# The opening of a grouped-convolution and scan kernel: weights folded ahead, x in small pieces on two queues, and lone edges in the first pairs

## The chip, the core and the metric

The kernel runs on one core of a Trainium2 chip, in float32. The metric is the device time of one execution in microseconds (us). Its engines are TensorE (PE, with its weight loads as PEld), VectorE (DVE), ScalarE (ACT), GpSimd (POOL) and SyncE (SP), which issues most DMAs; ScalarE's queue can issue DMAs too. All times in this document are us, most of them from the start of the span.

## The reference

x has 4 images of 128 channels, 96 by 96. It is group-normalised (32 groups over channels and pixels, no learned scale), read as four sequences (rows, rows backwards, columns, columns backwards), and each sequence goes through the same block. The four results are fused by one matrix and added to x.

```python
t = grouped1x1(x, in_proj_w, in_proj_b, 4)            # 128 -> 512
u, gate = t[:, :256], t[:, 256:]
u = depthwise_conv(silu(u), dw_w, taps=5)
s = ssm_in_w @ u                                      # 256 -> 32
a = 0.999 + 0.0009 * sigmoid(ssm_delta_w @ u + ssm_delta_b)
bb, cc = tanh(ssm_b_w @ u + ssm_b_b), tanh(ssm_c_w @ u + ssm_c_b)
h = exp(P) * cumsum(bb * s * exp(-P)), P = cumsum(log a)   # h = a * h + bb * s
u = u + ssm_out_w @ (cc * h + ssm_d * s)
u = grouped1x1(u * sigmoid(gate), mix_w, mix_b, 4)
y = out_proj_w @ u + out_proj_b                       # 256 -> 128
out = x + fuse_w @ concat(y of the 4 sequences) + fuse_b
```

## The kernel before

**Phases, steps, pairs, units.** The work is 8 phases: image 0 by columns ("V"), image 0 by rows ("H"), image 1, and so on. A phase runs two sequences of opposite direction at once (s = 0 and 1). It has 6 steps of 16 lines; each step is cut into 4 interleaved residues p, taken in the order `TURN = (1, 2, 3, 0)`. One residue of one sequence is a *unit* of 384 positions; the two units of a residue are a *pair* t, 24 to a phase and 192 in all. `pair(t)` issues the first `LAG` = 6 pairs, `pair_on(t)` the others, `tail()` the end. `start()` is the opening, up to the point where the first projection can be issued. In these functions the order of the code is the order on each engine (a manual schedule). The loads ahead of them (`load_x` with its statistics, the weights) are ordered by the scheduler.

**The opening.** x of image 0 arrives in pieces on SyncE's queue; each 384 columns (a chunk, 0.197 MB, 24 in all) get a `bn_stats` on VectorE (L329). `stats_first` then yields the normalisation step by step: aggregate, product with `gmean` for the group means, product for the variances, square root and reciprocal (`inv`), the scaled input weights `wn`, and their biases `bn` from products of the *scaled* weights with the means. Between its steps `start` issues fillers (L1163, products of x with itself that nobody reads) and the fold of the output weights: `outer` (L1170) forms fuse_w times out_proj_w for four directions (`w_of`), `inner` (L1178) multiplies mix_w in (`w_fin`). Three further products with vectors give the fused bias `b_fin` (L1252).

**In-projection and SiLU.** `burst(j, g)` is the in-projection of residue g: channel half j, both sequences; `silus(j, g)` its SiLU on ScalarE (L509). `sils[step]` holds the results of a step. For later steps `front(t + R)` in pair t does the same, one residue a pair, four pairs ahead. `load_front` refills `x_in` behind it, row by row as the in-projection has read them: `x_in` has one buffer per sequence.

**The depthwise convolution** of a unit: channel half 0 on TensorE (`conv` with the matrices `band`, then `conv_less` with `less` for the neighbouring columns, then a copy of the result to `u`, L904), channel half 1 as five `taps` on VectorE (L728) with the first on ScalarE (L726). For residues 0 and 3 the part of `conv_less` is a single tap (`alone(p)`); `pair_on` then calls `add_lone` instead: one VectorE instruction (L675) that adds the shifted edge rows from the tile `lone` to the convolution and writes `u`. `keep_lone` writes a step's edge rows (32 partitions, four DMAs) to DRAM, and `load_lone` reads them back in the other layout. Before, the pairs 0 to 5 always use `conv_less`.

**Projection, scan, output.** `proj` (L130 psum<-u,main) computes b, c, delta and s; the scan runs on VectorE one step later; `out_of` adds ssm_out to a copy of u that `under` put into PSUM; `gating` multiplies by the gate; `accumulate` applies `w_fin`. Phase 2 of an image reads back what phase 1 kept in DRAM: `keep_silu` writes the SiLU results of step 0 (four DMAs of 770 KB, one a residue), `kept` the gates.

**Statistics of the next image** come from chunks `xs` that `load_chunks` fetches and `stats_chunks` reads: before, one in each of the pairs 2 to 5, then two in every pair of residues 3 and 0.

**DMA order.** A DMA queue runs its transfers in order of issue. The program has eight DMA semaphores, used in turn over all queues: a ninth transfer is issued only when the one that had its semaphore has landed, and the issuing engine waits for that in its own order.

Of the kernel before, what the change touches and what calls it, by code (L numbers as in the profile page):

```python
# [42 lines left out]
F32 = mybir.dt.float32  # L43
# [4 lines left out]
P = 128  # L48
# [8 lines left out]
R = 4  # L57
# [11 lines left out]
def conv_preact_kernel(  # L69
# [95 lines left out]
    stats, free = {}, [FRONT[1]]  # L165
# [10 lines left out]
    def stats_first(b):  # L176
# [11 lines left out]
        gm4 = sp.tile([P, 4], F32, tag="gm4", name=f"gm4_{b}")  # L188
        nc.vector.tensor_scalar_mul(gm4, gmask, mean)
# [18 lines left out]
        stats[b] = (wns, bn)  # L208
        yield
        pb = bank(free[0])  # L210
# [114 lines left out]
    def load_x(chunks):  # L325
        for c, n in chunks:
            nc.sync.dma_start(accf[:, bass.ds(c * SC, n * SC)], xr[b0, :, bass.ds(c * SC, n * SC)])
            for e in range(c, c + n):
                nc.vector.bn_stats(stats_of(b0)[:, e, :], accf[:, bass.ts(e, SC)])  # L329
# [11 lines left out]
    nc.scalar.activation(first_table, first_table, AF.Sqrt)  # L341
    w_small = load(small, "small", nc.scalar)
    load_x([(0, 1), (1, 1), (2, 1), (3, 2), (5, 2), (7, 3), (10, 4), (14, 4), (18, 4), (22, 2)])
    w_out_fuse = shared()
    nc.sync.dma_start(w_out_fuse[:, 0 : 2 * HID + 4 * P], fuse)
# [36 lines left out]
    for s in range(2):  # L382
# [13 lines left out]
    nc.gpsimd.tensor_scalar_mul(b_proj[64:P, 0:1], b_proj[64:P, 0:1], 0.5)  # L396
    nc.gpsimd.tensor_scalar_mul(
        w_proj[:, :, 2 * MH : 3 * MH], w_proj[:, :, 2 * MH : 3 * MH], 0.5
    )
# [10 lines left out]

    def chunks_of(t):

        un = units[min(2 * t, NU - 2)]
        st, k = divmod(t % NP, R)
        if t < LAG:
            return [(b0 + 1, t - 2)] if t > 1 else []
        if un["order"] == "V" and un["b"] + 1 < B and k > 1:
            return [(un["b"] + 1, 4 * st + 2 * (k - 2) + e) for e in range(2)]
        return []
# [11 lines left out]
    def stats_chunks(t):  # L431
        for b, c in chunks_of(t):
            nc.vector.bn_stats(stats_of(b)[:, c, :], chunks.pop((b, c)))
# [914 lines left out]
```

## Time and profile before

| | |
|---|---|
| three runs | 1741.92, 1742.92, 1745.32; median 1742.92 |
| profiled execution | 1742.22 |
| its span | 1740.4 |
| granted TensorE clock | 1.0 throughout |
| TensorE, VectorE, ScalarE, GpSimd busy | 99%, 87%, 86%, 83% |
| first `bn_stats` | 3.64 |
| fillers | 11.64 to 20.38 |
| mean product on TensorE | 20.31 |
| first SiLU | 24.46 |
| projections of pairs 0 to 6 | 34.93, 41.81, 48.59, 56.03, 63.92, 70.68, 79.30 |

Rows of a timeline show start, length, engine, line, operation and tiles; x14 after a row is a count of equal instructions that follow each other. One float32 product shows as two passes, so that seven fillers are fourteen rows. A helper such as `mm` (L130) records most products, so they are told apart by their tiles: `psum<-u,main` is a projection, `psum<-sil,band` a convolution, `psum<-sil,less` its second part, `psum<-x_in,wn` an in-projection, and L539 a gate.

### The profile page before, as it was taken

Reading aid. Unit: us, or ns where it says so; the run is one execution under the profiler, and the core shown is the slowest. Engines: PE = TensorE matmul, PEld = TensorE weight load, DVE = VectorE, ACT = ScalarE, POOL = GpSimd, SP = SyncE. Lnnn points to the kernel's source line nnn. Section 1 sums busy time; section 2 is a strip of 40 time slices with the busy share of each in tenths; the row PEclk is TensorE's granted clock in tenths of the full one; section 3 lists DMA queues with packets and bytes.
Section 4 is the critical chain, followed back from the end, with each engine's and each line's share of the span. In section 5 each row is a group of like instructions: output and inputs, shape, how many; then the busy total and the mean of one; then the engine's idle time right before and its main releaser. Section 6 shows DMA issues by size and latency. Waiting matters only on the chain.

```text
span 1740.4 us, 54418 instructions
## 1 busy us (share of the span) xinstructions
PE 1719.8 (99%) x22662; PEld 648.0 (37%) x22662; DVE 1509.2 (87%) x1508; ACT 1494.9 (86%) x2543; POOL 1449.3 (83%) x1496
## 2 busy tenths in 40 slices
PE   7999999999999999999999999999999999999998
PEld 3333333333333433344333443334333343334333
DVE  6899988888889998888889999888888888888887
ACT  4788888889888898888988888888998888888875
POOL 3589889888778988988787988898878889887887
PEclk9999999999999999999999999999999999999999
DMA  7755965368984786337896488433897549743365
GB/s 240 220 160 199 291 189 158 109 218 272 283 276 154 244 277 199 117 122 244 267 304 232 149 301 255 147 120 133 287 287 251 179 138 294 213 136 133 146 227 166
DMA packets 175908, 362.68 MB, mean 208 GB/s; under 512 B 16688, under 2 KB 150320, under 8 KB 175664
## 3 DMA queue, kind: packets, MB, share of 16 engines
q1 hardware_dynamic: 175520, 359.17, 64.5%
q8 instruction: 179, 2.93, 0.7%
q14 instruction: 65, 0.53, 0.1%
q10 hardware_dynamic: 144, 0.04, 0.0%
HBM read 220.62 MB, written 138.53 MB: 206 GB/s over the span
## 4 chain that ended last, share of the span: by engine, by line
PE 93%; DVE 2%; POOL 2%; ACT 1%; DMA 1%; issue 1%; SPq 0%; POOLq 0%; DVEq 0%; ACTq 0%
PE psum L130 79%; PE psum L559 8%; PE psum L539 6%; DVE psum L728 1%; PE psum L1163 1%; POOL acc L859 1%; DMA acc<-in_xr 0%; DVE u L622 0%; POOL t L809 0%; ACT psum L573 0%; ACT psum L726 0%; DVE u L728 0%; ACT sil L509 0%; DMA edge<-sil 0%; POOL t L810 0%
## 5 line engine op out<-in xcount | busy, mean ns | idle before, releaser
L728 DVE SCALAR_TENSOR_TENSOR psum<-sil,small,psum 128x768 f32<-128x768 f32 x576 | 589.0, 1023 | 43.5 <-ACT psum L726 18.3
L130 PE MATMUL psum<-u,w_fin 128*32 128x384 f32 (+1 forms) x6192 | 541.6, 485 | 1.1 <-DVE acc L857 0.5
L130 PE MATMUL psum<-u,main 128*32 128x384 f32 x6144 | 535.1, 489 | 0.7 <-DVE u L904 0.6
L622 DVE SCALAR_TENSOR_TENSOR u<-gate,psum 128x768 f32<-128x768 f32 x376 | 341.7, 950 | 151.2 <-PE psum L559 49.6
L859 POOL TENSOR_TENSOR acc<-ys,acc 128x384 f32<-128x384 f32 x375 | 416.5, 1132 | 14.7 <-DMA acc<-in_xr 1.9
L809 POOL TENSOR_TENSOR t<-t,t 64x384 f32<-64x384 f32 (+1 forms) x192 | 282.2, 1470 | 72.3 <-DVE t L803 50.1
L130 PEld LDWEIGHTS psum<-u,w_fin 128*32 128x32 f32 x6192 | 196.4, 110 | 308.4 <-issue 234.5
L573 ACT COPY psum<-u 128x768 f32<-128x768 f32 x383 | 300.6, 799 | 11.4 <-DVE u L622 4.9
L130 PEld LDWEIGHTS psum<-u,main 128*32 128x32 f32 x6144 | 180.4, 110 | 323.3 <-issue 217.2
L130 PE MATMUL psum<-sil,band 128*32 128x384 f32 x3072 | 285.6, 489 | 0.0
L776 POOL TENSOR_SCALAR t<-tm 64x384 f32<-64x384 f32 x184 | 172.5, 938 | 116.1 <-ACT tm L765 104.0
L810 POOL TENSOR_TENSOR t<-t,t 64x384 f32<-64x384 f32 (+1 forms) x192 | 233.9, 1218 | 15.1
L777 POOL TENSOR_TENSOR t<-t,tm 64x384 f32<-64x384 f32 x192 | 211.2, 1100 | 28.4 <-ACT t L768 13.7
L559 PE MATMUL psum<-t,main 32*128 32x384 f32 x1536 | 229.0, 525 | 3.2 <-ACT psum L573 3.2
L726 ACT ACTIVATE psum<-sil,small 128x768 f32<-128x768 f32 x191 | 172.4, 903 | 67.0 <-DVE u L622 62.3
L728 DVE SCALAR_TENSOR_TENSOR u<-sil,small,psum 128x768 f32<-128x768 f32 x192 | 194.9, 1015 | 6.8
L509 ACT ACTIVATE sil<-psum,bnorm 128x385 f32<-128x385 f32 x384 | 191.8, 584 | 4.6 <-PE psum L130 2.2
L539 PE MATMUL psum<-x_in,wn 32*128 32x384 f32 x768 | 164.0, 500 | 0.0
L842 ACT COPY ys<-psum 128x384 f32<-128x384 f32 x286 | 131.5, 477 | 28.8 <-PE psum L130 25.1
L130 PEld LDWEIGHTS psum<-sil,band 128*32 128x32 f32 x3072 | 88.8, 108 | 171.9 <-issue 63.0
L765 ACT ACTIVATE tm<-psum,small 128x384 f32<-128x384 f32 x192 | 110.9, 578 | 15.8 <-PE psum L130 6.6
L559 PEld LDWEIGHTS psum<-t,main 32*128 32x128 f32 x1536 | 94.6, 183 | 75.8 <-issue 41.2
(109 smaller groups left out, 1527.3 us busy)
## 6 DMA issues: line engine op xcount, KB each, us to landing
gate<-kept SPq DMA_DIRECT2D x114, 768.0 KB, 5.9
kept<-gate SPq DMA_DIRECT2D x74, 768.0 KB, 3.6
sil<-sil SPq DMA_DIRECT2D x64, 770.0 KB, 7.6
lone<-edge SPq DMA_DIRECT2D x39, 770.0 KB, 8.3
x_in<-in_xs SPq DMA_DIRECT2D x250, 96.2 KB, 3.3
edge<-sil SPq DMA_DIRECT2D x96, 192.5 KB, 4.3
out<-acc SPq DMA_DIRECT2D x46, 384.0 KB, 7.3
acc<-in_xr SPq DMA_DIRECT2D x39, 384.0 KB, 6.8
```

Source lines behind the costliest of these rows:

```text
L130: nc.tensor.matmul(o[r, : rhs.shape[-1]], lhsT, rhs, start=start, stop=stop, skip_group_check=True)
L509: nc.scalar.activation(sils[step][:, s, j, g, :], bank(bk)[:, : N + 1], AF.Silu, bias=bn[:, 1:2] if j else bn[:, 4 + g : 5 + g],)
L539: nc.tensor.matmul(bank(to)[:, :N], stats[un["b"]][0][r, s, :], x_in[s][r, q, off : off + N], start=True, stop=True)
L559: nc.tensor.matmul(bank(ssm(bi, s) + j)[:, :N], w_so[r, bass.ts(j, P)], z[r, :], start=(bi, s) not in seeded, stop=True, skip_group_check= ...
L573: nc.scalar.copy(psum[:, ssm(bi, s) : ssm(bi, s) + 2, :N], us[bi][:, s])
L622: nc.vector.scalar_tensor_tensor(v, g, 1.0, pz, ALU.add, ALU.mult)
L728: nc.vector.scalar_tensor_tensor(us[i][:, :, 1, :] if k == K - 1 else part, src, w_tap[:, k : k + 1], part, ALU.mult, ALU.add,)
L776: nc.gpsimd.tensor_scalar(*decay(i))
L777: nc.gpsimd.tensor_mul(ta[0:64, p, :], tb[0:64, :], tm[0:64, :])
L809: engine.tensor_mul(ta[0:64, p, r], tb[64:P, r], ta[64:P, p, r])
L810: engine.tensor_add(tb[0:64, r], ta[0:64, p, r], tb[0:64, r])
L859: adder.tensor_add(part, y, part)
```

## The change

The change has two parts.

In the opening: `fuse` is loaded first, by ScalarE's queue; x comes in 15 pieces of one or two chunks, in turn by SyncE and ScalarE, with the small weights after the fourth. `outer` and `inner` stand at the front of `start`, two directions a bank, and ScalarE copies their results. Four fillers stand ahead of the mean product (seven before), one and the three products of `b_fin` between mean and variance product. The biases are products of the *unscaled* weights with mean x inv. The order of bursts, SiLUs, taps and convolution in `start` is new.

In the pairs: `keep_lone(0)` and `load_lone(0)` stand at the end of `start`, and the pairs 2 and 3 use `add_lone`. `keep_silu(0, g)` moves from the end of `start` into the pairs 0, 1 and 2. `under` no longer leaves out unit pair 0. The chunks of image 1 move from the pairs 2 to 5 to the pairs 5 and 20 to 22 (three in 22).

```diff
 def stats_first(b):
...
-        wn = wns[:, 0, :]
+        shift = sp.tile([P, 1], F32, tag="dev", name=f"shift_{b}")
+        nc.vector.tensor_mul(shift, mean, inv[:, 0:1])
+        pb = bank(free[0])
+        for g in range(4):
+            for q in range(R):
+                mm(pb[:, 4 + g : 5 + g], q, w_in[0:32, 0, 32 * g : 32 * g + 32], shift[0:32, :], True, True)
...
-        product(pb[:, 0:4], wn, gm4)
-        for g in range(4):
-            for q in range(R):
-                mm(pb[:, 4 + g : 5 + g], q, wn[0:32, 32 * g : 32 * g + 32], mean[0:32, :], True, True)
-        nc.vector.tensor_sub(bn, b_in, pb[:, 0:8])
+        product(pb[:, 0:4], w_in[:, 0, :], gm4)
+        nc.vector.tensor_sub(bn[:, 0:4], b_in[:, 0:4], pb[:, 0:4])
...
+    def load_x(ends):
+        for e, (c, to) in enumerate(zip([0] + ends, ends)):
+            cols = bass.ds(c * SC, (to - c) * SC)
+            (nc.scalar if e % 2 else nc.sync).dma_start(accf[:, cols], xr[b0, :, cols])
+            if e == 3:
+                load_small()
+            for k in range(c, to):
+                nc.vector.bn_stats(stats_of(b0)[:, k, :], accf[:, bass.ts(k, SC)])
...
-    nc.sync.dma_start(w_out_fuse[:, 0 : 2 * HID + 4 * P], fuse)
+    nc.scalar.dma_start(w_out_fuse[:, 0 : 2 * HID + 4 * P], fuse)
+    load_x([1, 2, 3, 4, 6, 8, 10, 12, 14, 16, 18, 20, 22, 23, 24])
...
+        if ph == 0:
+            places = singles[2:] * 2 + [LAG - 1, NP - 4, NP - 3, NP - 2]
...
     def under(bi, s):
-        if bi + s == 0:
-            return
...
     def pair(t):
-            conv(i, banks)
-            conv_less(i, banks, False)
-            for s in range(2):
-                nc.vector.tensor_copy(us[i][:, s, 0, :], bank(min(banks) + s)[:, :N])
+            single = alone(units[i]["p"])
+            conv(i, banks, single)
+            if single:
+                add_lone(i, banks)
+            else:
+                conv_less(i, banks, False)
+                for s in range(2):
+                    nc.vector.tensor_copy(us[i][:, s, 0, :], bank(min(banks) + s)[:, :N])
...
-        if t == 2:
-            keep_lone(0)
...
+        for g in {0: (0,), 1: (1, 2), 2: (3,)}.get(t, ()):
+            keep_silu(0, g)
...
     def start():
+        nc.scalar.activation(first_table, first_table, AF.Sqrt)
+        outer((0, 1), 2)
+        outer((2, 3), 3)
+        inner((0, 1), 4)
+        inner((2, 3), 5)
...
-        for n in (512, 512, 512):
-            filler(n)
-        next(pieces)
         for n in (512, 512, 512, 512):
             filler(n)
         next(pieces)
-        outer(0, 0, nc.scalar.copy)
-        outer(1, 1, nc.scalar.copy)
         next(pieces)
-        outer(2, 4, nc.scalar.copy)
+        filler(512)
+        pf = bank(3)
...
-        inner((0, 1), 0)
-        inner((2, 3), 1)
...
-        for g in range(R):
-            keep_silu(0, g)
...
+        keep_lone(0)
+        load_lone(0)
```

What the edit does to the order on the engines shows at three places. First ScalarE from the program's first instruction to the first SiLU; `acc` is x, `shared` holds the fuse weights and their fold. Before:

```order
L322 DMA small<-in_small 128x86
L341 ACT_TABLE_LOAD
L341 ACTIVATE first_table<-first_table 128x1
L1174 COPY shared<-psum 128x256 x2
L198 ACTIVATE std<-var_253 128x2
L200 ACT_TABLE_LOAD
L200 ACTIVATE first_table<-std 128x1
L1174 COPY shared<-psum 128x256
L509 ACTIVATE sil_293<-psum,bnorm_266 128x385 x16
```

And now:

```order
L348 DMA shared<-in_fuse 128x1024
L330 DMA acc<-in_xr 128x384 x2
L324 DMA small<-in_small 128x86
L330 DMA acc<-in_xr 128x768 x4
L330 DMA acc<-in_xr 128x384
L1200 ACT_TABLE_LOAD
L1200 ACTIVATE first_table<-first_table 128x1
L1189 COPY shared<-psum 128x512 x2
L1198 ACTIVATE w_fin<-psum 128x512 x2
L1219 ACTIVATE b_fin<-psum,small 128x1
L196 ACTIVATE std<-var_276 128x2
```

Nine transfers now stand ahead of the table load and of the first copy of the fold. Then TensorE over the same stretch, before:

```order
L1163 MATMUL psum<-acc 128x512 x7
L130 MATMUL psum<-mv_221,gmean 32x1 x4
L1170 MATMUL psum<-shared 128x128 x4
L130 MATMUL psum<-ex_235,gmean 32x1 x8
L1170 MATMUL psum<-shared 128x128 x4
L1163 MATMUL psum<-acc 128x128
L130 MATMUL psum<-gm_0_237,wn_263 32x4 x4
L130 MATMUL psum<-mean_231,wn_263 32x1 x16
```

And now (`mv` and `ex` are the inputs of the mean and the variance product, `shift` is mean x inv):

```order
L1185 MATMUL psum<-shared 128x128 x8
L1193 MATMUL psum<-shared 128x128 x8
L1178 MATMUL psum<-acc 128x512 x4
L130 MATMUL psum<-mv_251,gmean 32x1 x4
L1178 MATMUL psum<-acc 128x512
L1218 MATMUL psum<-small,shared 128x1 x3
L130 MATMUL psum<-ex_261,gmean 32x1 x8
L130 MATMUL psum<-shift_283,main 32x1 x16
```

The fold moved ahead of the fillers; a filler and the bias products took its place between the mean and the variance product. Last, SyncE's queue from the end of `start` into the pairs, before:

```order
L489 DMA sil_0_202<-sil_293 512x1x385
L489 DMA sil_1_203<-sil_293 512x1x385
L489 DMA sil_2_204<-sil_293 512x1x385
L489 DMA sil_3_205<-sil_293 512x1x385
L427 DMA xs_0_437<-in_xr 128x384
L297 DMA x_in_70<-in_xs 32x385
L297 DMA x_in_71<-in_xs 32x385
```

And now:

```order
L672 DMA edge_0_212<-sil_308 32x4x385 x4
L678 DMA lone_440<-edge_0_212 128x4x385
L299 DMA x_in_70<-in_xs 32x385
L299 DMA x_in_71<-in_xs 32x385
L317 DMA x_in_70<-in_xs 64x385
L503 DMA sil_0_204<-sil_308 512x1x385
L299 DMA x_in_70<-in_xs 32x385
L299 DMA x_in_71<-in_xs 32x385
L317 DMA x_in_71<-in_xs 64x385
L503 DMA sil_1_205<-sil_308 512x1x385
L503 DMA sil_2_206<-sil_308 512x1x385
```

The four edges and the read of `lone`, which waits for them, stand in front of the `sil` writes, and these stand between the loads of `x_in` for step 2.

More of the change, by code (lines that the diff above doesn't have):

```diff
@@ L1191, in start @@
         next(pieces)
[L1192 to L1193 removed]
         next(pieces)
[L1195 removed]
+        filler(512)
+        pf = bank(3)
+        terms = [(w_of[:, 0, j, :], b_mix[:, j : j + 1]) for j in range(2)] + [(w_fuse[:, 0, :], b_out)]
+        for i, (lhsT, rhs) in enumerate(terms):
+            nc.tensor.matmul(pf[:, 0:1], lhsT, rhs, start=(i == 0), stop=(i == len(terms) - 1))
+        nc.scalar.activation(b_fin, pf[:, 0:1], AF.Identity, bias=b_fuse)
         next(pieces)
[L1197 to L1200 removed]
+        next(pieces)
         sils[0] = wk.tile([P, 2, 2, 4, N + 1], F32, tag="sil", name="sil_0")
```

106 lines of the change are left out of this document (50 added, 56 removed).

## The prediction

> **What bounds the kernel now.** All times are us from the start of the span. I read the page first: its busy times and the shares of the chain that ended last.
>
> ```profile
> PE 1719.8 (99%) x22662; PEld 648.0 (37%) x22662; DVE 1509.2 (87%) x1508; ACT 1494.9 (86%) x2543; POOL 1449.3 (83%) x1496
> PE 93%; DVE 2%; POOL 2%; ACT 1%; DMA 1%; issue 1%; SPq 0%; POOLq 0%; DVEq 0%; ACTq 0%
> ```
>
> TensorE is busy for 99% of the span and carries 93% of the chain, so whatever lets its queue run earlier in the opening comes off the end, unless TensorE has to wait again behind it. The diff touches the opening and pairs 0 to 6, so next came the chain of waits over the first 80 us (start, length, what):
>
> ```profile
> 3.62 7.98 DMA acc<-in_xr
> 11.64 8.73 PE psum L1163 x14
> 55.43 0.56 DVE u L904
> 59.37 3.60 DMA x_in<-in_xs
> 63.11 3.60 PE psum L130 x48
> ```
>
> x loads until 11.60 (a part of it; the rest hides), then seven fillers of two passes each hold TensorE until 20.37, with the product of the means right behind. From there the chain is TensorE's own but for two places: in pair 3 it waits for the copies of u, and in pair 4 for x_in, which lands at 59.37 + 3.60 = 62.97. Then the windows by stage: mean product to first SiLU, first SiLU to first projection, and pair by pair, each from its projection to the next (window, length, PE, PEld, DVE, ACT, POOL, clock, DMA share, GB/s).
>
> ```profile
> 20.31:24.46 4.15, 4.15 (x107) 3.62 (x114) 2.18 (x11) 2.69 (x6) 0.00 (x0) 1.00 0.79 185
> 24.46:34.93 10.47, 10.47 (x202) 5.78 (x184) 6.17 (x17) 8.98 (x19) 3.17 (x4) 1.00 0.35 89
> 34.93:41.81 6.88, 6.88 (x104) 2.30 (x100) 5.70 (x7) 5.83 (x11) 1.94 (x2) 1.00 1.05 288
> 41.81:48.59 6.78, 6.78 (x104) 2.19 (x100) 5.03 (x7) 5.61 (x12) 3.13 (x3) 1.00 1.09 201
> 48.59:56.03 7.44, 6.81 (x104) 2.15 (x100) 5.33 (x8) 4.99 (x10) 3.17 (x3) 1.00 0.86 252
> 56.03:63.92 7.89, 7.48 (x100) 2.23 (x100) 6.76 (x9) 6.90 (x13) 3.12 (x3) 1.00 0.84 233
> ```
>
> TensorE fills every window but 0.6 of the fifth and 0.4 of the sixth. From 34.93 on the transfers are nearly saturated too (share 0.84 to 1.09), and that second bound decides this forecast.
>
> **Part 1, up to the mean product (20.31 now).** The statistics and TensorE's fillers must both be over. In the answers below are the statistics, four weight loads of the fillers, SyncE's waits before an issue, ScalarE's table load and copies, and the second fold product.
>
> ```profile
> 11.62 6.67 DVE L329 BATCH_NORM_STATS2 bn<-acc 128x6 f32<-128x384 f32 x14 [0.41 <-DMA acc<-in_xr]
> 18.32 0.81 DVE L178 BATCH_NORM_AGGREGATE mv<-bn 128x2 f32<-128x144 f32 x1
> 10.00:11.00 1.00, 0.00 (x0) 0.00 (x0) 1.00 (x3) 0.00 (x0) 0.93 (x3) 1.00 1.03 418
> 15.22 0.33 PEld L1163 LDWEIGHTS psum<-acc 128*128 128x128 f32 x1 [0.52 <-issue]
> 16.07 0.33 PEld L1163 LDWEIGHTS psum<-acc 128*128 128x128 f32 x1 [0.52 <-issue]
> 16.78 0.19 PEld L1163 LDWEIGHTS psum<-acc 128*128 128x128 f32 x1 [0.38 <-issue]
> 17.21 0.19 PEld L1163 LDWEIGHTS psum<-acc 128*128 128x128 f32 x1 [0.24 <-issue]
> SPq L315 <- DMA acc<-in_xr: 4.6, 4, 1.4
> 1.25 1.28 ACT L341 ACT_TABLE_LOAD   x1 [1.25 <-PEq L1330]
> 21.29 0.76 ACT L1174 COPY shared<-psum 128x256 f32<-128x256 f32 x2 [18.54 <-PE psum L1170]
> 27.29 2.05 PE L1178 MATMUL psum<-shared 128*128 128x128 f32 x16
> ```
>
> Statistics: VectorE does its last 14 chunks without a gap at 6.67 / 14 = 0.48 each, and data comes at 0.42 MB/us, 0.47 per chunk of 0.197 MB: both rates are equal. Smaller pieces save idle time in front, but the 0.52 MB of fuse now go first. I take the last chunk at 18.1 instead of 18.29 (bounds 17.2 and 19.4, the latter with all of fuse, 1.25, in front) and the mean product possible at 18.1 + 0.81 + 0.1 = 19.0.
>
> Fillers: the fold moves ahead of them, and ScalarE now issues transfers before its copies. The row of L315 shows what an issue costs when eight transfers are out: it waits for an older landing. ScalarE's last one waits so for chunks 12 and 13. With fuse, twelve chunks and the small weights, 2.93 MB, ahead of them against 2.80 MB for the landing at 11.60, that is 11.9 at worst and 10.1 if the transfers run at 0.41 from 2.0 on; I take 10.8. Then issue (0.4), table load (1.28), Sqrt and the first copy of twice the width (0.6): 13.3. Only then can the second fold product start. A pass costs 0.85 early (15.22 to 16.07) and 0.43 later (16.78 to 17.21); the pace turned after 5 us of work (11.64 to 16.7). The first fold product (from some 5 to 8.5) is too early to keep it so. Second product: 2 x 2.05 at the slow pace, 13.3 to 17.1; fillers slow until 18.3 (1.4 passes), then 6.6 x 0.43: the mean product at 21.1, +0.8. Bounds 19.0 (statistics decide) and 22.6.
>
> The Trainium skill (TensorE: Matmul & The Clock Gate, Part 1) has the clock open after about 3.4 us of work; this trace took 5. By the page all eight passes would be fast and the product would come at 20.5, 0.6 earlier.
>
> **Part 2, mean product to first projection.**
>
> ```profile
> 20.48 1.16 PE L1170 MATMUL psum<-shared 128*128 128x128 f32 x8
> 21.57 0.30 PE L130 MATMUL psum<-ex,gmean 128*32 128x1 f32 x16
> 23.12 0.25 PE L130 MATMUL psum<-gm,wn 128*32 128x4 f32 x8
> 24.46 7.73 ACT L509 ACTIVATE sil<-psum,bnorm 128x385 f32<-128x385 f32 x16 [0.34 <-PE psum L130]
> 30.37 1.02 DVE L724 TENSOR_SCALAR psum<-sil,small 128x768 f32<-128x768 f32 x1
> 32.96 0.83 PE L1252 MATMUL psum<-small,shared 128*128 128x1 f32 x6
> ```
>
> Between the mean and the variance product stood 1.26 (20.31 to 21.57) with four fold products (1.16) as cover; now a filler (2 x 0.43) and the three bias products (0.83) stand there, 1.8: +0.55, paid in full. The bias product of 0.25 in front of the in-projections goes: -0.25. First SiLU at 24.46 + 0.8 + 0.55 - 0.25 = 25.55, +1.1. From there ScalarE's 16 SiLUs (0.48 each) set the pace. Now the first tap starts 5.9 after the first SiLU though its ten SiLUs take 4.8: w_fin's evacuation was in its way; and the fold (2.05) and the bias products (0.83) stand in TensorE's queue. All three are gone: 9.35 instead of 10.47 (bounds 9.2 and 10.2). First projection at 34.9, as now: the opening's losses and gains cancel.
>
> **Part 3, pairs 1 to 3.**
>
> ```profile
> 40.04 0.88 PE L130 MATMUL psum<-sil,less 64*32 64x384 f32 x16
> 41.01 1.02 DVE L904 COPY u<-psum 128x384 f32<-128x384 f32 x2
> 41.81 2.79 PE L130 MATMUL psum<-u,main 128*32 128x384 f32 x32
> 44.53 0.92 PE L539 MATMUL psum<-x_in,wn 32*128 32x384 f32 x4
> 45.38 1.50 PE L130 MATMUL psum<-sil,band 128*32 128x384 f32 x16
> DVE bn L433 <- DMA xs<-in_xr: 2.0, 1, 2.0
> ```
>
> A group's rows overlap the next by 0.07, so conv_less is 0.81, a projection 2.72, the gates 0.85, a convolution 1.43. Pairs 2 and 3 lose conv_less and get add_lone, one VectorE instruction of about 1.0 (as both copies of u together), which is longer than the in-projection that covers it, so that TensorE waits some 0.3 for it: 6.3 instead of 6.78 (bounds 6.0 and 6.8). Pair 3 loses the wait for xs as well, since its statistics moved: 6.3 instead of 7.44. With 6.85 for pair 1, pair 3 projects at 34.9 + 6.85 + 6.3 + 6.3 = 54.35, and TensorE wants pair 4's in-projection 2.72 + 0.85 + 1.43 + 0.81 = 5.8 later, at 60.15, its second half 0.5 after that: 2.4 ahead of 63.11.
>
> **Part 4, what is late next: x_in.**
>
> ```profile
> 26.39 5.65 SPq L297 DMA_DIRECT2D x_in<-in_xs  x8
> sil<-sil SPq DMA_DIRECT2D x4, 770.0 KB, 11.2
> edge<-sil SPq DMA_DIRECT2D x4, 192.5 KB, 4.2
> lone<-edge SPq DMA_DIRECT2D x1, 770.0 KB, 4.6
> ```
>
> SyncE's queue is now: x_in for step 1, four edges, lone, then the four sil writes among small loads. The edges go out behind x_in, 7.6 after the first SiLU (26.39 + 5.65 - 24.46): 33.1. lone reads what they wrote, so SyncE stops until they land (four issues, 4.2: some 5.6), then 4.6 for lone: 43.3. Behind it, in one ring, come 3.15 MB of sil, 0.79 of kept, 0.8 of x_in, gates and xs, and x_in for pair 4 (0.5): 5.24 MB at the mean of 288 and 201 GB/s of the two saturated windows is 21.4, so 64.7; kept's long rows go faster, I take 64.3 (62 to 67). The sil writes started at 33.7 before, ahead of everything. The second half of pair 4's in-projection starts at 64.4 instead of 63.11: +1.3. So TensorE waits 4.2, and what pairs 2 and 3 gave is taken back. add_lone itself needs lone behind pair 2's convolution, at 34.9 + 6.85 + 2.72 + 0.85 + 1.43 = 46.75: 3.4 to spare.
>
> Behind pair 4 nothing of size: one ScalarE copy for a VectorE add in pair 6, and three chunks (0.48 each) in pairs 20 to 22, where VectorE, 87% busy, has the room; phases 1 to 7 are the same. Sum: +1.3.
>
> The profiled execution took 1742.22 (span 1740.4, 1.8 around it) and lies 0.7 below the median 1742.92; 1742.92 + 1.3 = **1744.2**.
>
> **Rivals.**
> 1. The transfers keep up: x_in lands before 60.2 and TensorE keeps its lead. 63.11 becomes 60.7: 1740.5. For it: the DMA share leaves some holes at 48 to 64 (0.84). Against: 5.24 MB in 17 us would be 0.31 MB/us, which no window here reaches for such rows.
> 2. Slower: the clock falls in TensorE's new wait in pair 4. The price is the fillers' start: six passes at 0.85 instead of 0.43 are 2.6 lost, so 1746.8, and 1748.8 if x_in is also 2 later. It decides from the length of wait at which the clock falls; in this trace 11.6 idle left it slow and 0.6 didn't. The page named above puts that at one idle window of about 3.4, which the 4.2 expected would reach if it holds a whole window.
> 3. The fold is not held up by ScalarE's queue, so the statistics decide (19.0): everything from there on, the edges too, 2.1 earlier: 1742.1. The Trainium skill (DMA: Bandwidth & Descriptors, "Issuing engines are not separate DMA queues") speaks against it: a second queue saves issue time, no bandwidth; with fuse in front the statistics would then end at 19.4 and this would give 1743.4.
>
> **How the numbers follow.** Forecast 0.45, rival 1 0.14, rival 2 0.20, rival 3 0.16, other losses (lone late, a cold array already in the in-projections) 0.05. 0.2% (3.5 us, about what a measurement of this kernel can tell from no change) reaches from 1739.4 to 1746.4. Faster than that is half of rival 1 and tails of 3 and the forecast: 0.11. Slower is two thirds of rival 2, the rest and a tail: 0.19. Range: rival 1 with a little of rival 3 below, 1739.9; rival 2 with a late x_in above, 1748.6.
>
> **What would show it.** In the profile after: ScalarE's copies of the first fold at about 12.7 to 14, fillers until after 20.5, mean product at 21, first SiLU at 25.5, first projection within 0.5 of 34.9, pairs 2 and 3 at about 6.3 each, and TensorE idle before pair 4's in-projection for a DMA of x_in landing at 64. Wrong if that wait is under 1.5, if the first SiLU comes before 24.3, or if fillers run at 0.85 a pass after pair 0.

## The result, and the profile after

| | before | after |
|---|---|---|
| median of seven runs each | 1742.92 (1741.35 to 1745.32) | 1747.35 (1744.17 to 1749.66) |
| ratio, 95% interval | | 1.002 (1.0010 to 1.0029) |
| profiled execution, its span | 1742.22, 1740.4 | 1748.18, 1746.3 |
| its mean granted clock | 1.0 | 0.995 |

The change makes the kernel slower by 0.1 to 0.3%. The forecast was 1744.2 with a range of 1739.9 to 1748.6: the range holds the result, but the way there holds one large error. The same points of the program as forecast and as measured, each in its own row:

| | before | forecast | after |
|---|---|---|---|
| mean product | 20.31 | 21.1 | 20.91 |
| first SiLU | 24.46 | 25.55 | 25.09 |
| first projection | 34.93 | 34.9 | 39.21 |
| projections of pair 0 to pair 3 | 21.10 | 19.45 | 19.45 |
| pair 3 to pair 4 | 7.89 | 10.86 | 10.15 |
| pair 4 to pair 8 | 34.20 | 34.20 | 35.56 |
| projection of pair 8 | 98.12 | 99.41 | 104.37 |

(10.86 is the forecast's second half at 64.4, plus the 0.81 that lie before between it and the projection, less 54.35.) At pair 8 the kernel is 6.25 behind the one before; the spans differ by 5.9, so all of it happens in the first 100 us. The page of the kernel after, busy times and shares of the chain:

```profile
PE 1724.1 (99%) x22624; PEld 650.0 (37%) x22624; DVE 1502.3 (86%) x1504; ACT 1497.5 (86%) x2545; POOL 1451.9 (83%) x1496
PE 94%; DMA 1%; DVE 1%; ACT 1%; POOL 1%; issue 1%; SPq 0%; ACTq 0%; DVEq 0%; POOLq 0%
```

TensorE does fewer instructions than before (22624 against 22662) and is busy 4.3 longer, which points to slower work and not to more of it.

The windows by stage of the kernel after answer to those of before: mean product to first SiLU, first SiLU to first projection, then pair by pair (window, length, PE, PEld, DVE, ACT, POOL, clock, DMA share, GB/s).

```profile
20.91:25.09 4.18, 3.27 (x85) 2.37 (x92) 1.73 (x10) 1.95 (x4) 0.00 (x0) 0.99 0.78 182
25.09:39.21 14.12, 14.12 (x188) 4.72 (x172) 5.94 (x17) 8.96 (x17) 0.00 (x0) 0.52 0.45 110
39.21:46.14 6.93, 6.93 (x105) 2.34 (x100) 4.89 (x6) 6.00 (x11) 1.93 (x2) 1.00 0.67 210
46.14:52.40 6.26, 6.03 (x89) 2.00 (x85) 5.36 (x7) 5.91 (x12) 3.12 (x3) 1.00 0.49 130
52.40:58.66 6.26, 5.93 (x84) 1.90 (x85) 5.00 (x6) 5.48 (x11) 3.12 (x3) 1.00 1.07 280
58.66:68.81 10.15, 7.54 (x100) 2.38 (x100) 8.03 (x9) 5.88 (x12) 3.13 (x3) 1.00 1.01 287
68.81:77.27 8.46, 8.46 (x105) 2.61 (x101) 3.50 (x5) 4.76 (x10) 3.10 (x3) 0.80 0.75 255
```

Two rows carry the loss. The second stage takes 14.12 instead of 10.47. TensorE shows as busy in all of it, yet its clock column says 0.52: it does the same work at half pace. And before pair 4's projection TensorE is idle for 2.6 of 10.15, after which the clock column falls again, to 0.80. Only the rows of pairs 2 and 3, 6.26 each, are the gain that was meant. The chain of waits of the kernel after (start, length, what) has the pieces in the order of time:

```profile
13.02 3.78 PE psum L1193 x16
16.80 4.18 PE psum L1178 x8
23.93 18.08 PE psum L130 x263
51.04 9.58 DMA sil<-sil
60.64 6.36 DMA x_in<-in_xs
67.14 6.16 PE psum L130 x64
```

The second fold product, the fillers, then TensorE's own products from 23.93 on; and at 60.64 a load of x_in that could be issued only when a sil write had landed. Why the clock fell, the timeline of TensorE shows (start, length, engine, line, operation, tiles, count, idle time ahead in brackets):

```profile
22.05 0.72 PE L1218 MATMUL psum<-small,shared 128*128 128x1 f32 x6
22.70 0.31 PE L130 MATMUL psum<-ex,gmean 128*32 128x1 f32 x16
23.93 0.43 PE L130 MATMUL psum<-shift,main 32*32 32x1 f32 x32 [0.91 <-DVE shift L202]
26.91 6.98 PE L130 MATMUL psum<-x_in,wn 32*32 32x385 f32 x96
33.82 2.79 PE L130 MATMUL psum<-sil,band 128*32 128x384 f32 x16
```

Between the variance product and the biases TensorE has nothing to do for 0.91, and on both sides of it stand products of one column. Before, four fold products and a filler stood there. The trace's record of the clock changes at 18.18 (open), 25.01 (half), 38.66 (open), 69.38 (half) and 72.80 (open): all distances are multiples of 3.413; one such stretch of 3.413 is called a step of the clock here. The record begins with its first entry, and ahead of that the clock column says 1.00 even where the fillers run at the slow pace; so "1.0 throughout" for the kernel before holds from 16.63 on, where its record begins. Windows cut at these times, and at 21.59, one such step ahead of the fall:

```profile
18.18:21.59 3.41, 3.41 (x16) 1.41 (x15) 1.77 (x5) 0.00 (x0) 1.62 (x4) 1.00 1.08 210
21.59:25.01 3.42, 2.51 (x76) 1.91 (x82) 1.48 (x9) 1.95 (x4) 0.00 (x0) 1.00 0.72 175
25.01:38.66 13.65, 13.65 (x177) 4.72 (x172) 5.94 (x17) 8.64 (x17) 0.00 (x0) 0.50 0.43 107
```

One window with 2.51 busy of 3.42, much of it one-column products, and four steps of half clock follow it. The Trainium skill (TensorE: Matmul & The Clock Gate, Part 1) has the gate judge by a free-running window of 3.413 us; the distances above agree. It has the clock fall after an idle window; here 0.91 of idle time was enough.

### The profile page after: what moved, and what is told of

The parts are those of the page before. It is cut to its first block, busy times and chain, and to the rows that moved or that the text cites. A ratio compares the mean times of both kernels' runs of the same rounds, so it can differ in the third digit from the quotient of the medians.

```text
span 1746.3 us, 54356 instructions
## 1 busy us (share of the span) xinstructions
PE 1724.1 (99%) x22624; PEld 650.0 (37%) x22624; DVE 1502.3 (86%) x1504; ACT 1497.5 (86%) x2545; POOL 1451.9 (83%) x1496
## 4 chain that ended last, share of the span: by engine, by line
PE 94%; DMA 1%; DVE 1%; ACT 1%; POOL 1%; issue 1%; SPq 0%; ACTq 0%; DVEq 0%; POOLq 0%
PE psum L130 80%; PE psum L573 8%; PE psum L553 6%; DVE psum L740 1%; DMA acc<-in_xr 1%; DMA sil<-sil 1%; DMA x_in<-in_xs 0%; DVE u L634 0%; PE psum L1178 0%; ACT psum L585 0%; POOL t L821 0%; DVE u L740 0%; PE psum L1193 0%; ACT psum L738 0%; POOL acc L871 0%
## 5 line engine op out<-in xcount | busy, mean ns | idle before, releaser
L871 POOL TENSOR_TENSOR acc<-ys,acc 128x384 f32<-128x384 f32 x375 | 422.7, 1149 | 14.7 <-DMA acc<-in_xr 2.8
```

Of the source, the lines that this page charges most:

```text
L871: adder.tensor_add(part, y, part)
```

## The experiments

The kernel before ran beside them in three groups, with medians of 1743.31 (the first four runs), 1743.62 (warm_gap, warm_inproj, fold_late, fold_back) and 1743.74 (the others); each ratio is taken within its group. Each kernel has one profile, so what the rows show is one execution of it.

**The two parts apart.** pairs_only has the opening of before and the pairs of after, opening_only the reverse.

For the first, the diff is the lines of the change on the pairs, on the kernel before:

```diff
+            places = singles[2:] * 2 + [LAG - 1, NP - 4, NP - 3, NP - 2]
...
+            single = alone(units[i]["p"])
+            conv(i, banks, single)
...
+        for g in {0: (0,), 1: (1, 2), 2: (3,)}.get(t, ()):
+            keep_silu(0, g)
...
+        keep_lone(0)
+        load_lone(0)
```

> The pair part of the change alone, on the opening of before: lone edges in pairs 2 and 3, the sil writes in pairs 0 to 2, the chunks moved. Theory (x_in queued behind the sil writes is what pair 4 waits for): first projection near 34, pairs 2 and 3 about 6.3 each, x_in lands near 64, TensorE waits about 4 in pair 4 and the clock may close for one window after it: 1744 to 1746.5. Rival (the late x_in in the kernel after is only a result of its late opening): the pairs keep their gain of 2.4 and it takes about 1740.5.

For the second it is these lines undone, on the kernel after:

```diff
-            single = alone(units[i]["p"])
-            conv(i, banks, single)
+            conv(i, banks)
...
-        keep_lone(0)
-        load_lone(0)
+        for g in range(R):
+            keep_silu(0, g)
```

> The opening of the change alone, with the pairs of before. Theory (the loss sits in the opening, where the clock closes during the in-projections): clock at half from about 25 to 38, first projection near 39.2 as in the kernel after, time 1746.5 to 1748.5. Rival (the opening is harmless and the pairs lose the time): 1742 to 1743.5.

pairs_only: 1745.44, ratio 1.0008 (0.9997 to 1.0020). opening_only: 1745.81, ratio 1.0009 (1.0000 to 1.0019). Windows of pairs_only, pair 3 to pair 4 and pair 4 to pair 5:

```profile
55.13:65.22 10.09, 7.83 (x100) 2.37 (x101) 7.97 (x9) 6.31 (x13) 3.33 (x4) 0.98 1.03 295
65.22:73.45 8.23, 8.23 (x103) 2.46 (x101) 3.56 (x5) 4.42 (x9) 3.18 (x3) 0.82 0.75 249
```

and of opening_only from the clock's fall to its return:

```profile
24.69:38.34 13.65, 13.65 (x176) 5.08 (x168) 6.25 (x19) 8.79 (x18) 0.00 (x0) 0.50 0.32 90
```

By the medians each part costs about 2 alone (2.1 and 2.5), and together about what the whole costs (4.4); but the first interval takes in no change at all and the second begins at it, so the sizes are rough, and the rows are the better evidence. The pairs bring their own wait (2.1 idle before pair 4's in-projection) and a fall of one step behind it; the opening brings its own four steps at half clock, its first projection at 39.70. So there are two losses, and each comes without the other.

**Both kinds of cover.** after_warm adds a filler behind the variance product and five among the in-projections.

```diff
         next(pieces)
+        filler(512)
         next(pieces)
...
+        filler(256, 0)        # and four more, ahead of later bursts
         burst(0, 2)
```

> The kernel after with one filler of 512 columns more between the variance product and the bias products, and five of 256 among the in-projections of the opening; nothing else. Theory (the clock closes because the fold no longer stands among the in-projections): clock 1.0 from 18 to 64, first projection at 34.5 to 35.5 instead of 39.2, then a wait for x_in of about 4 in pair 4: 1743 to 1746. Rival (TensorE's order and the waits for ScalarE set the first projection, not the clock): it stays at 39 or gets later by the fillers' 2 us, 1747 to 1750.

1747.48, ratio 1.0022 (1.0014 to 1.0031). Its windows: first SiLU to first projection, pair 3 to pair 4, and the two steps of half clock that begin in that:

```profile
24.30:36.33 12.03, 12.03 (x199) 3.99 (x182) 5.90 (x17) 9.17 (x18) 0.00 (x0) 1.00 0.37 92
55.61:66.53 10.92, 8.40 (x101) 2.46 (x101) 8.77 (x10) 6.09 (x13) 3.13 (x3) 0.87 1.03 297
63.80:70.63 6.83, 6.64 (x60) 2.01 (x64) 4.66 (x5) 2.02 (x4) 0.00 (x0) 0.50 0.96 309
```

The clock stays open and the first projection comes 2.9 earlier, yet the time is that of the kernel after: the wait in pair 4 (2.51) is now followed by two steps of half clock instead of one.

**One sil write instead of four.** after_one_sil leaves out three of the four writes of phase 0's SiLU results.

```diff
-        for g in {0: (0,), 1: (1, 2), 2: (3,)}.get(t, ()):
-            keep_silu(0, g)
+        if t == 0:
+            keep_silu(0, 0)
```

> The kernel after with three of the four sil writes of phase 0 left out (step 5 reads the first in their place, so the second half of phase 0 works on other data): 2.4 MB less ahead of x_in. Theory (pair 4 waits for x_in behind these writes): the wait of 2.6 and the closed window behind it are gone, 1743.5 to 1745. Rival (lone, edges and kept alone fill the queue): a wait of over 1.5 remains, 1746.5 to 1748.

1744.31, ratio 1.0004 (0.9995 to 1.0012). Pair 3 to pair 4, and the fall in the opening:

```profile
57.87:64.78 6.91, 6.91 (x101) 2.30 (x101) 4.89 (x6) 5.32 (x11) 3.13 (x3) 1.00 0.62 167
23.51:37.16 13.65, 13.65 (x186) 5.08 (x175) 6.30 (x20) 8.88 (x18) 0.00 (x0) 0.50 0.33 85
```

With 2.3 MB less in the queue the four loads of x_in for pair 4 land at 59.3 to 63.5 instead of 66.4 to 67.8, pair 4 does not wait, and no clock falls behind it: 3.0 of the kernel after are gone. The opening is as it was.

**Which cover counts.** Theory A: the in-projections are too little work by themselves. Theory B: the window with the idle time ahead of them. warm_gap has only the first filler of after_warm, warm_inproj only the five others.

```diff
         next(pieces)
+        filler(512)
         next(pieces)
         sils[0] = wk.tile([P, 2, 2, 4, N + 1], F32, tag="sil", name="sil_0")
```

> The changed kernel with one filler of 512 columns between the variance product and the bias products, and nothing else. Theory A (the in-projections alone are too little work for the clock; before, the fold products stood among them): the clock falls all the same, at most a window or two of 3.41 later, and the first projection comes at 37.5 to 39.5 (39.21 in the changed kernel); time 1745.5 to 1747.5. Theory B (the 0.91 of idle time with one-column products ahead of the in-projections closes it): the clock stays open from 18 on and the first projection comes at 34.5 to 35.5; time 1743 to 1744, with pair 4's wait still there.

```diff
+        filler(256, 0)
         burst(0, 2)
...
+        filler(256, 2)
         burst(1, TURN[0])
...
+        filler(256, 6)
         burst(1, TURN[1])
...
+        filler(256, 4)
         burst(1, TURN[2])
...
+        filler(256, 2)
         burst(1, TURN[3])
```

> The changed kernel with five fillers of 256 columns among the in-projections, and none ahead of the bias products. Theory A: the clock stays open and the first projection comes at 36 to 36.5 (36.33 with both kinds of filler); time within 0.7 of the kernel with both, 1747.5. Theory B: the clock falls at about 25 as in the changed kernel; the first projection comes at 38 to 40.

warm_gap: 1744.44, ratio 1.0004 (0.9995 to 1.0012). warm_inproj: 1755.38, ratio 1.0072 (1.0060 to 1.0085). Windows of warm_gap, cut at the clock's steps (the one with the filler, and two with in-projections and the start of the convolution), and its pair 3 to pair 4:

```profile
22.10:25.52 3.42, 3.42 (x82) 2.25 (x88) 1.37 (x8) 1.95 (x4) 0.00 (x0) 1.00 0.57 144
25.52:28.93 3.41, 3.30 (x92) 1.40 (x75) 0.62 (x8) 3.39 (x8) 0.00 (x0) 1.00 0.03 5
28.93:32.34 3.41, 3.34 (x48) 1.03 (x48) 1.81 (x5) 3.41 (x9) 0.00 (x0) 1.00 0.52 134
55.80:65.73 9.93, 7.52 (x100) 2.37 (x100) 7.81 (x9) 5.86 (x12) 3.13 (x3) 1.00 1.04 282
```

and the fall in warm_inproj:

```profile
24.21:44.69 20.48, 20.48 (x170) 6.21 (x170) 6.13 (x19) 9.03 (x18) 0.00 (x0) 0.50 0.22 55
```

Theory A falls. With one filler in the gap the clock stays open, and a step that holds hardly more than in-projections (25.52 to 28.93) does not make it fall. Five fillers behind the gap do not open a clock that has fallen: it stays at half for six steps, until 44.69, the fillers themselves run at half pace, and the first projection comes at 46.27. B was right on the fall but had warm_inproj's first projection at 38 to 40. In warm_gap's profile pair 4's wait of 2.40 is there, and the clock did not fall behind it. That wait lay across two steps of 3.41, 1.4 in one and 1.0 in the next; but so did the kernel after's (1.4 and 1.2), where the clock fell, so this does not explain it.

**The same in the kernel before.** fold_late moves the second fold product, with the sums on GpSimd that follow it, out of the in-projections. uncovered moves the two fold products that stand between the variance product and the biases in among the in-projections, and leaves the small filler beside them out.

```diff
-        inner((0, 1), 0)
-        inner((2, 3), 1)
...
             keep_silu(0, g)
+        inner((0, 1), 0)
+        inner((2, 3), 1)
```

> The kernel before with only this changed: the second fold product, its evacuation and the sums on GpSimd stand behind the second part of the first convolution and the last tap, not among the in-projections. Theory A: the clock falls in the opening of this kernel too, for one window of 3.41 or more, and the first projection comes at 36.5 to 39 (34.93 before); time 1745 to 1747. Theory B: the idle time ahead of the in-projections is covered as before, the clock stays open, and the first projection comes at 34.9 to 35.9 (the fold product is mostly hidden under the wait for u); time 1743 to 1744.3.

```diff
-        outer(2, 4, nc.scalar.copy)
         next(pieces)
-        outer(3, 5, nc.vector.tensor_copy)
-        filler(128)
...
+        outer(2, 0, nc.vector.tensor_copy)
+        outer(3, 1, nc.vector.tensor_copy)
         inner((0, 1), 0)
         inner((2, 3), 1)
```

> The kernel before with only this changed: the fold products of directions 2 and 3 and the small filler, which cover the time between the variance product and the bias products, stand among the in-projections, ahead of the second fold product. Theory B (one window with this idle time and one-column products closes the clock, and in-projections don't open a closed one): the clock falls at 23 to 27 for 6.8 to 13.7, the first projection comes at 38 to 40 instead of 34.93, time 1745.5 to 1748. Theory A (only work among the in-projections counts, and there is now more of it): the clock stays open, first projection at 34.9 to 36, time 1743 to 1744.5.

fold_late: 1749.07, ratio 1.0034 (1.0021 to 1.0046). uncovered: 1748.20, ratio 1.0026 (1.0014 to 1.0037). uncovered, the step ahead of the fall, and the time at half clock:

```profile
21.21:24.62 3.41, 2.37 (x81) 1.95 (x88) 1.81 (x10) 2.43 (x5) 0.18 (x1) 1.00 0.85 202
24.62:34.86 10.24, 10.24 (x111) 7.58 (x95) 1.70 (x10) 6.12 (x12) 0.39 (x1) 0.50 0.23 61
```

The idle time in front of the biases is 1.04 here, and the clock falls in the old kernel as it does in the new one: first projection 41.12 (a part of that is the moved products themselves, which now stand in TensorE's way). It opens again behind a step filled with fold products of 128 rows (30.52 to 35.53), after one step fewer than in the kernel after, and falls once more for a step at 82.64. Four of its six runs have a clock of 0.996 or 0.997 and 1748.1 to 1750.4, two have 1.0 and 1744.1 and 1744.8, so it seems that the same instructions do not always make it fall (those two were not profiled).

fold_late tells less than it should. The rows of its step ahead of the fall and of the half clock:

```profile
22.08:25.49 3.41, 3.02 (x86) 1.79 (x93) 1.24 (x7) 2.40 (x5) 0.00 (x0) 1.00 0.67 167
25.49:35.73 10.24, 10.24 (x127) 4.05 (x112) 5.54 (x14) 7.27 (x15) 0.00 (x0) 0.50 0.41 113
```

The step ahead of the fall holds the same instructions as in the kernel before, so the moved product cannot have caused this fall, at most let it last. What that step has and the profile of before has not is a wait of 0.39 for x_in, behind a mean product at 19.85 instead of 20.31. The move also brought a wait of 1.98 of its own, the bias products for GpSimd's sums, and behind it a second fall from 42.56 to 45.97; the first projection came at 42.44, later than either theory had it. The run does not decide between them.

**The fold back among the in-projections**, with the cover in the gap kept and eight fillers ahead of the mean product.

```diff
-        inner((0, 1), 4)
-        inner((2, 3), 5)
...
-        for n in (512, 512, 512, 512):
+        for n in (512,) * 8:
             filler(n)
...
         silus(0, 3)
+        inner((0, 1), 0)
+        inner((2, 3), 1)
```

> The changed kernel with the second fold product back among the in-projections (VectorE evacuates it), the bias products behind the first convolution as before, eight fillers ahead of the mean product instead of four and one behind the variance product. That the second fold product was late because ScalarE issued transfers first, and held up the fillers: the mean product comes at 19.8 to 20.2, when the statistics are over, instead of 20.91; first SiLU 23.5 to 24.3. Theories A and B both: the clock stays open and the first projection comes at 33.8 to 35.2. Pair 4's wait for x_in stays (2 to 5, since TensorE is early and x_in is not), with a fall of the clock behind it: time 1744.3 to 1746. If the time is that of the changed kernel (1747.4), the opening's loss is not what makes the end later.

1747.19, ratio 1.0021 (1.0010 to 1.0032). Pair 3 to pair 4, and the half clock that begins in it:

```profile
54.56:65.23 10.67, 8.45 (x100) 2.41 (x100) 8.56 (x9) 6.18 (x13) 3.13 (x3) 0.89 0.97 283
62.91:69.74 6.83, 6.83 (x64) 1.75 (x48) 4.50 (x5) 2.43 (x5) 0.00 (x0) 0.50 0.96 286
```

The opening is mended (first projection 35.28, expected 33.8 to 35.2), the time is not: the fillers, which read a chunk of x that lands at 11.98, ended at 20.68, so the mean product came at 20.61 and not at 20; and pair 4's wait was paid with two steps of half clock.

**Both losses taken away.** both_mended is warm_gap with one sil write instead of four.

```diff
+        filler(512)              # behind the variance product
...
+        if t == 0:
+            keep_silu(0, 0)      # instead of four
```

> The changed kernel with the one filler of 512 columns behind the variance product, and with one of the four sil writes of phase 0 instead of four (left out: step 5 reads the first in place of the other three, so part of the output is not the reference's). If the changed kernel loses by two things, the clock in the opening and pair 4's wait: no fall of the clock anywhere, first projection at 36.5, pair 4's wait under 0.5, pair 4's projection at 62.5 to 63, pair 8's at 96.3 to 97; time 1741 to 1742.5. If the write is what the time depends on and the opening not: as with one write alone, 1744.3.

1740.51, ratio 0.9984 (0.9976 to 0.9993). First SiLU to first projection, and pair 3 to pair 4:

```profile
24.98:35.29 10.31, 10.08 (x188) 3.35 (x172) 5.79 (x17) 9.47 (x19) 0.00 (x0) 1.00 0.43 109
54.57:61.41 6.84, 6.84 (x100) 2.25 (x100) 4.82 (x6) 5.25 (x11) 3.14 (x3) 1.00 0.67 179
```

No fall anywhere, pair 8's projection at 95.28 (2.8 ahead of the kernel before), and the only time of this study that is surely below the kernel before. It does less than the reference asks for, so it is no candidate. Against the kernel before of the same group the kernel after lies 4.4 above, warm_gap 0.8, after_one_sil 1.0, and both_mended 3.2 below: mending the gap alone gives 3.6, the writes alone 3.4, both 7.7. The cleanest step is the one filler on top of after_one_sil, 1744.31 to 1740.51. So the two losses are enough to explain why the change is slower; how much of the 3.2 comes from writes that the kernel before has to make and this one leaves out is not shown.

**ScalarE without the transfers.** act_free is warm_gap with ScalarE issuing only fuse, two pieces of x and the small weights, and its table load ahead of the last three.

```diff
-            (nc.scalar if e % 2 else nc.sync).dma_start(accf[:, cols], xr[b0, :, cols])
+            (nc.scalar if e % 2 and e < 4 else nc.sync).dma_start(accf[:, cols], xr[b0, :, cols])
```

> The kernel with the one filler behind the variance product, and ScalarE issuing only fuse, two pieces of x and the small weights, with its table load ahead of the last three; SyncE issues the other pieces. Forecast's step (ScalarE's waits before an issue hold the copies of the fold, and these the second fold product and the fillers): first copy of the fold at 9.2, second fold product from 9.8, mean product at 19.6 to 20.2, when the statistics are over, instead of 21.29; first projection about 1 earlier than 36.52, the rest lost again in pair 4's wait: time 1743.5 to 1744.5 against 1744.4. If something else makes the fold late: second product from 13, mean product at 21.

1749.22, ratio 1.0040 (1.0026 to 1.0054). Timeline of TensorE and of ScalarE's first copy:

```profile
9.13 0.59 ACT L1190 COPY shared<-psum 128x512 f32<-128x512 f32 x1 [1.06 <-PE psum L1186]
8.88 2.94 PE L1194 MATMUL psum<-shared 128*128 128x128 f32 x16
19.09 0.29 PE L130 MATMUL psum<-mv,gmean 128*32 128x1 f32 x8 [3.84 <-DVE mv L178]
```

and the half clock:

```profile
17.77:38.25 20.48, 19.16 (x226) 8.08 (x234) 9.41 (x29) 10.06 (x20) 4.23 (x8) 0.50 0.53 118
```

The prediction's step is shown: without the waiting issues ahead of the table load and the copies, the second fold product starts at 8.9 instead of 13.0, and the statistics decide the mean product, at 19.09, where the prediction had put that case (19.0). But the fillers now end at 15.26, TensorE is idle for 3.84, and the clock falls there for six steps: the slowest but one of all.

**A version from what was learned.** six_fillers is the kernel before with a filler less (they ended 1.2 after the statistics) and the chunks of image 1 moved as in the change.

```diff
-        for n in (512, 512, 512):
+        for n in (512, 512):
             filler(n)
...
+            places = singles[2:] * 2 + [LAG - 1, NP - 4, NP - 3, NP - 2]
```

> The kernel before with six fillers ahead of the mean product instead of seven, and the chunks of image 1 moved as in the changed kernel; sil writes, pairs and the rest as before. Statistics are over at 19.13 and the fillers end at 20.38 before, so the mean product comes at 19.5; pair 3 loses its wait of 0.63 for xs, pair 4 most of its 0.41 as TensorE is early and x_in 1 to 2 earlier: 1.4 to 2 earlier in all, 1741.3 to 1742 against 1743.4. Against it: with a filler less the clock opens later in some runs, or pair 4 waits longer for x_in and the clock falls there: 1743 to 1746.

1742.62, ratio 0.9997 (0.9987 to 1.0007): no difference that can be measured. The profiled run, in the step ahead of a fall and behind it:

```profile
22.55:25.96 3.41, 2.95 (x94) 1.56 (x102) 0.49 (x5) 2.33 (x7) 0.00 (x0) 1.00 0.63 153
25.96:32.78 6.82, 6.82 (x72) 4.86 (x58) 0.93 (x5) 4.29 (x10) 1.51 (x2) 0.50 0.29 75
```

The mean product came at 19.47 as expected, but the first in-projections then waited 0.46 for x_in, and in this run the clock fell; seven of its eleven runs lie at 1741.1 to 1742.7, four at 1744.1 to 1746.8. No complete kernel of this study beats the one before.

## Why the prediction was right, and where it was wrong

The direction and the range came out, the middle of the way did not: 4.4 slower instead of 1.3. That the range still holds it is luck. Its upper end was set for a fall of the clock in pair 4 together with a late x_in; most of what filled it is a fall of the clock in the opening, which had no price.

**Right, with its sizes: up to the first SiLU.** ScalarE's waits hold its table load:

```profile
ACT L1200 <- DMA acc<-in_xr: 11.0, 1, 11.0
12.40 1.05 ACT L1189 COPY shared<-psum 128x512 f32<-128x512 f32 x2
```

The first row is of the kernel after's waits (total, times, longest), the second of its timeline. The fold's second product ran from 13.02 to 16.80 (forecast 13.3 to 17.1), the clock opened at 18.18 (18.3), the mean product stood at 20.91 (21.1), and mean to variance product took 1.79 (1.8). One sum there is off: 13.3 and twice 2.05 are 17.4, not 17.1, which would put the mean product at 21.3; the second product took only 3.78, so the 17.1 came out all the same. That the fold was late because of ScalarE's issues was argued in the prediction; act_free shows it. Rival 3 is out: the fold was held up, and where act_free made the rival's condition, the time rose all the same, as the clock fell while TensorE waited 3.84 for the statistics.

**Right, with its sizes: pairs 1 to 3.** 6.93, 6.26 and 6.26 against 6.85, 6.3 and 6.3.

**Wrong: first SiLU to first projection**, 9.35 with bounds of 9.2 and 10.2, measured 14.12. This is the mis-sized term. The prediction read the fold products, the filler and the bias products ahead of and among the in-projections as cost alone; the ones in front of the biases were also the cover that kept TensorE's clock. 14.12 less the 10.31 of both_mended, 3.8, is the clock (3.1 by the 10.98 of warm_gap). The other 1.0 is there with the clock open too, and is a second term that the prediction put at nothing. Of the last in-projection ahead of the first projection, the first row is the kernel before, the second the later part of it in both_mended:

```profile
33.72 1.28 PE L130 MATMUL psum<-x_in,wn 32*32 32x385 f32 x32
33.91 1.45 PE L130 MATMUL psum<-x_in,wn 32*32 32x385 f32 x24 [0.17 <-DMA x_in<-in_xs]
```

In both_mended this in-projection starts at 32.89, 7.91 after the first SiLU instead of 9.26: the saving is there, 1.35. But a quarter into it the rest of x_in has not landed, it goes on at 33.91, and the projection follows 2.40 after its start instead of 1.21. The saving was lost to the refill of x_in, the same kind of wait as in pair 4. The case of a cold array in the in-projections was named, in a share of 0.05 and with no price.

**Right in kind, smaller in size: pair 4.** TensorE waited for x_in:

```profile
PE psum L130 <- DMA x_in<-in_xs: 2.6, 1, 2.6
```

2.6 instead of 4.2 (3.75 by the prediction's own times, 64.4 less the 60.65 at which it has the second half wanted). The piece of x_in it waited for landed at 60.64 + 6.36 = 67.0, 2.7 later than forecast, while the clock had made the first projection 4.3 later: most of the shorter wait is TensorE's own delay. The transfers were not faster than put there: the first edge went out at 34.94 instead of 33.1, and x_in landed 32.1 behind it, forecast 31.2. In pairs_only, where the opening keeps its clock, the wait is short too (2.1); there the transfers were faster than forecast, 30.1 from the first edge to x_in. Pair 3 to pair 4 took 10.15 instead of 10.86. pairs_only and after_one_sil show that the sil writes in front of x_in are the cause. Rival 1, in which x_in keeps up, is out.

**Rival 2 came as well.** The clock fell behind that wait, for one step of 3.41, and pair 4 to pair 8 took 35.56 instead of 34.20 (33.87 in both_mended, without a wait): 1.4 to 1.7 instead of the 2.6 that rival 2 gave. The prediction took it for an alternative to its forecast, though the forecast's own wait made it likely.

Altogether: 4.3 at the first projection, nothing in pairs 1 to 3, -0.7 in pair 4 and 1.4 behind it are the 5.0 by which pair 8 came later than the forecast (104.37 against 99.41). Some 0.3 of it is gone at the end of the span, the profiled execution is 0.8 above the median of the kernel after, and the one before was 0.7 below its own, so the median misses by 3.15 and not by 5.

## What to carry to other kernels

Before work is taken off a matrix engine that waits anyway, ask what its clock will see: cover that looks like padding can be what keeps the clock, and the price of losing it (3.1 to 3.8 here, by stage) is larger than the idle time that it covered (0.9). Read the clock column beside the busy column, since a busy engine at half clock looks like one that is bound. And when an opening is made earlier, look at the next transfer that is not: its gain went into the refill of x_in ahead of the first projection, and the gain of the pairs was lost again at pair 4's load of x_in in every complete kernel that kept the pairs' change.

## What the runs showed of the hardware that was not expected

- The clock falls for far less than a whole idle step. Steps with 2.51 of 3.42 (after), 2.37 of 3.41 (uncovered) and even 2.95 of 3.41 busy (six_fillers), with one-column products among them, were each followed by a fall, and so was one with 3.02 of 3.41 (fold_late). A step of little but in-projections with 3.30 of 3.41 (warm_gap) was not, nor the next, 3.34 with the start of the convolution. Nor was one with 1.98 of 3.41 (after, 62.55 to 65.96, ahead of pair 4), so the busy share alone does not decide.
- A fallen clock is not opened by work that would hold an open one. In-projections (tiles of 32 rows), which fill TensorE's row wholly, left it at half from 25.01 until the convolution behind them (33.82; open at 38.66); with five fillers of 128 rows among them it stayed at half for 20.48. It came back with the convolution or the fold (128 rows). That the rows in use are what is counted is a reading of these cases and was not tried by itself.
- The kernel before stands near this edge itself. Of its 76 runs beside the experiments, 13 have a mean clock of 0.998 or less, and all of these took 1745.5 or more; of the others all but one took less than that. What decides from run to run was not settled; the steps lie at another place of the program in each profile (in before, after, warm_gap and both_mended the clock opens for good or for its first long stretch at 16.63, 18.18, 18.69 and 17.45), which could do it and was not tested.
- A mean clock below 1 need not mean a fall that costs something. In the profiles of warm_gap, after_warm, after_one_sil and fold_back the first fold product opened the clock for one step, too early to last: in warm_gap from 8.45 to 11.86, then half until 18.69. The mean counts that half, but not the slow time ahead of the first entry.
- Whether a wait of 2.1 to 2.6 in pair 4 makes the clock fall for none (warm_gap), one (after, pairs_only, act_free) or two steps (after_warm, fold_back) varied in the same way. It is what parts warm_gap from after_warm, whose median is 3.0 higher with the same first projection and nearly the same wait: with two steps of half clock pair 3 to pair 4 took 10.92 instead of 9.93, and pair 4 to pair 8 35.88 instead of 33.87. Why the clock fell in one and not in the other is left open.
